# Opening an accumulation bank with its own first products, and new ranks in a list scheduler, in a four-layer attention, convolution and scan kernel

## The chip, the cores and the metric

The kernel runs on one core of a Trainium2 chip. The metric is the device time of that core in microseconds (us), as the median of several executions. "TensorE" (PE in the profile, its weight loads PEld) is the matrix engine, "VectorE" is DVE, "ScalarE" is ACT, "GpSimd" is POOL, and "SyncE" is SP.

## The reference, cut to what matters

```python
x = L0(x)   # self-attention over 4096 positions, q and k of 16 channels; gamma * out + x
x = L1(x)   # two 3x3 convolutions with 4-bit quantized weights and activations
x = L2(x)   # selective scan: 256 channels x 16 states, h = exp(dt*A)*h + dt*B*x, y = sum_n C_n*h_n,
            # gating, projection, group norm over the whole image, silu, + x
x = L3(x)   # self-attention over 4096 positions, q, k, v of 64 channels; x + wo @ out
```

There are four images of 128 channels and 64 x 64 positions. Each image passes the layers in this order, but different images can be in different layers at once. The kernel uses that: while one image is in the scan, which keeps VectorE busy, another is in an attention, which keeps TensorE and ScalarE busy.

## The kernel before

The program decides the instruction order of every engine on the host, with a list scheduler. Each piece of work is a chain (a Python generator) that yields one operation at a time with its engine, an estimated time and what it needs. The scheduler takes the operation with the smallest key and writes it out. On the chip, every engine then runs its instructions in exactly that order and waits where something is not yet there.

```python
class Order:
    LOAD, HOP, RANK = 1.3, 0.2, 0.15
    def run(self):
        ...
                load = self.LOAD if table not in (None, self.table) else 0.0
                key = start + load + self.RANK * item[0]      # item[0] is the chain's rank
                if best is None or key < best[0]:
                    best = key, start, load, item
```

So a rank is worth 0.15 us: it decides near-ties. The chains that this argument touches are these (cut):

```python
def exponentials():                  # ScalarE: p = exp(e), two halves per attention step t
    ... yield op("ACT", 1.02, ("e", t), *need, table="exp")
def decays(h):                       # ScalarE: da = exp(dt * A_n), what the scan of VectorE needs
    ... yield op("ACT", 0.7, ("dt", g), *need, table="exp")
def scans():                         # VectorE: ud*B (1.25), *C of the state before (1.22), two scans (1.26 each)
    ...
def preparation():                   # per scan group of 512 positions: products on TensorE, then on
    ...                              # ScalarE copies, silu, |x|, relu, exp, ln, with table loads
def products():                      # TensorE: values and sums of a bank
            for h in range(2):
                need = [("evict", k0 - 1)] if q == 0 and h == 0 else []
                time = (1.93 if layer == 0 else 0.95) + (0.3 if need else 0.0)
                yield op("PE", time, ("exp", t, h), *need)
                if need:
                    us = uss[k0] = ps_u.tile([P, 2, CB], F32, tag="us", name="us")   # one bank: values, sums
                    d = P if layer == 0 else 32
                    for m in range(P // d):            # the zero products
                        nc.tensor.matmul(flat(us)[m * d : (m + 1) * d, :], lhsT=w3[:, 0, m * d : (m + 1) * d],
                                         rhs=zero.to_broadcast([P, TB]), start=True, stop=False)
                ...
                        nc.tensor.matmul(us[rows, 0, :], lhsT=vts[s][:, 8 * q + k, cols],
                                         rhs=ps[t, h][:, k % 2, k // 4, :], start=False, stop=False)
            ...  # then the sums: lhsT=ones, into us[32 * m : 32 * m + 32, 1, :], start=False
```

There are 8 stages (two attentions of four images) of 16 banks and 64 attention steps t each, so 128 banks and 512 steps. The scan has 32 groups of 16 states, so 512 scan steps.

## Time and profile before

| | before |
|---|---|
| median of 3 runs | 3715.52 us (3714.67 to 3716.05) |
| profiled span | 3718.9 us |
| scan stretch: first product of the scan to the end of the last scan | 242.9 to 3361.4, 3118.5 us |
| ahead of it / after it | 242.9 us / 357.5 us |
| VectorE busy in the scan stretch | 2893.5 us, so idle for 225.0 us |

The page of the profile gives busy time per engine and, in 40 equal slices, the busy share of each in tenths. The chain that ended last follows the run back from its last instruction, each time to what released it. A view of waits has lines of the form "engine, its tile and line, <- what ended the wait: us in total, times, longest". The prediction below shows the lines of before that it reads. One more view of before, which it did not show, became the important one. It is VectorE's waits in the scan stretch:

```profile
DVE rall L647 <- PE sc L638: 66.3, 43, 3.8
DVE hs L1026 <- ACT da L991: 53.7, 34, 8.4
DVE hs L1008 <- ACT hlast L1001: 33.8, 36, 3.0
```

VectorE waits for TensorE's small products that turn the sums of attention into a column (sc), for ScalarE's decays (da), and for ScalarE's copy of the last state (hlast).

### The profile page before, as it was taken

To read this page: it belongs to the slowest core of one execution; us is meant where nothing else is said; L and a number is where in the kernel's file an instruction comes from. 1 tells how busy PE (TensorE), PEld (TensorE's weight loads), DVE (VectorE), ACT (ScalarE), POOL (GpSimd) and SP (SyncE) were. 2 spreads that over 40 slices of the span, in tenths; PEclk is the share of its full clock that TensorE was granted. 3 is DMA by queue.
4 is the path that set the end of the run, shared out by engine and by line. 5 is a ranking of instruction groups with operands and counts; after the bars stand their busy time and mean duration, and the time that the engine had idled before them with its cause. 6 is when DMAs were issued, how large, how long until landed. Compare 5 with 4: busy or idle time off the path is not lost.

```text
span 3718.9 us, 70774 instructions
## 1 busy us (share of the span) xinstructions
PE 3406.0 (92%) x29874; PEld 2235.8 (60%) x29879; DVE 3104.3 (83%) x2944; ACT 2513.0 (68%) x3656; POOL 1314.1 (35%) x568
## 2 busy tenths in 40 slices
PE   5999979989989999999888999999899989998998
PEld 3776656666666666655545666665555545565665
DVE  3369999999999999899988999999789888893333
ACT  3467767777787777777677767767777777774443
POOL 0014434444434444344433444443344444441000
PEclk8999999999999999999999999999999999999999
DMA  2023334333443334443443333343434444331000
GB/s 70 1 53 96 91 103 100 90 95 92 117 102 97 94 87 95 112 107 101 106 114 102 89 91 92 88 112 87 107 95 108 119 91 108 101 104 63 13 19 17
DMA packets 203658, 327.82 MB, mean 88 GB/s; under 512 B 50609, under 2 KB 53441, under 8 KB 203329
## 3 DMA queue, kind: packets, MB, share of 16 engines
q1 hardware_dynamic: 196384, 322.09, 34.7%
q8 instruction: 236, 3.87, 0.4%
q10 hardware_dynamic: 6944, 1.10, 0.2%
q14 instruction: 94, 0.76, 0.1%
HBM read 304.27 MB, written 18.87 MB: 87 GB/s over the span
## 4 chain that ended last, share of the span: by engine, by line
PE 61%; DVE 21%; ACT 10%; issue 5%; DMA 2%; ACTq 0%; SPq 0%; DVEq 0%
PE us L571 25%; PE e L494 14%; DVE hs L1026 9%; PE us L591 7%; DVE hs L1018 4%; DVE hs L1008 3%; PE conv L686 2%; ACT da L991 2%; ACT p L513 2%; PE xh L775 2%; PE sc L651 2%; PE yo L905 1%; PE sc L638 1%; PE proj L465 1%; PE proj L423 1%
## 5 line engine op out<-in xcount | busy, mean ns | idle before, releaser
L1043 POOL TENSOR_TENSOR y<-y,hs 128x1024 f32<-128x1024 f32 x512 | 1215.3, 2374 | 2050.1 <-DVE hs L1008 2033.6
L571 PE MATMUL us<-p,v 128*32 128x256 f32 (+1 forms) x12288 | 1521.7, 389 | 128.3 <-ACT p L513 128.1
L571 PEld LDWEIGHTS us<-p,v 128*32 128x32 f32 (+1 forms) x12288 | 1009.0, 138 | 550.1 <-ACT p L513 153.5
L513 ACT ACTIVATE p<-e 128x1024 f32<-128x1024 f32 x1024 | 1002.0, 1019 | 383.2 <-PE e L494 255.5
L1026 DVE TENSOR_TENSOR_SCAN hs<-da,hlast,hs 128x512 f32<-128x512 f32 x896 | 1102.3, 1264 | 45.5 <-ACT da L991 45.2
L991 ACT ACTIVATE da<-dt,amat 128x512 f32<-128x512 f32 x1024 | 701.1, 690 | 266.8 <-DVE hs L1026 263.0
L1008 DVE TENSOR_TENSOR hs<-hs,bc 128x1024 f32<-128x1024 f32 x512 | 666.9, 1303 | 34.7 <-ACT hlast L1001 33.8
L1018 DVE TENSOR_TENSOR hs<-ud,bc 128x1024 f32<-128x1024 f32 x512 | 656.9, 1283 | 0.0
L494 PE MATMUL e<-it,v 64*128 64x256 f32 x4096 | 534.6, 402 | 9.2 <-ACT p L513 8.2
L494 PEld LDWEIGHTS e<-it,v 64*128 64x128 f32 x4096 | 386.9, 193 | 155.6 <-issue 89.6
L591 PE MATMUL us<-p,ones 128*32 128x256 f32 x7040 | 469.9, 385 | 0.0
L591 PEld LDWEIGHTS us<-p,ones 128*32 128x32 f32 x7040 | 202.4, 110 | 183.6 <-issue 64.5
L535 DVE TENSOR_TENSOR acc<-p 128x1024 f32<-128x1024 f32 x24 | 29.4, 1225 | 225.4 <-PE us L591 192.6
L494 PEld LDWEIGHTS e<-it,j 64*128 64x128 f32 x2048 | 141.5, 190 | 101.9 <-issue 69.1
L494 PE MATMUL e<-it,j 64*128 64x256 f32 x2048 | 196.5, 310 | 5.1 <-ACT p L513 3.4
L1001 ACT COPY hlast<-hs 128x2 f32<-128x2 f32 x448 | 85.4, 191 | 130.9 <-DVE hs L1026 129.1
L535 DVE TENSOR_TENSOR acc<-p,acc 128x1024 f32<-128x1024 f32 x96 | 117.4, 1223 | 61.6 <-ACT p L513 58.1
L1026 DVE TENSOR_TENSOR_SCAN hs<-da,hs 128x512 f32<-128x512 f32 x128 | 149.9, 1204 | 8.6 <-ACT da L991 8.5
L775 PEld LDWEIGHTS <-w 128*128 128x128 bf16 x576 | 51.4, 98 | 98.3 <-issue 54.3
L775 PE MATMUL xh<-x,w 128*128 128x512 fp8e4 x384 | 95.3, 385 | 1.1 <-ACT sz L798 0.4
L1047 POOL TENSOR_TENSOR y<-y,sz 128x1024 f32<-128x1024 f32 x32 | 95.2, 2976 | 2.5
L465 PE MATMUL proj<-L_conv_wvT,x_in 128*128 128x128 f32 (+1 forms) x512 | 67.7, 288 | 22.9 <-DVE it L410 13.2
(162 smaller groups left out, 2617.3 us busy)
## 6 DMA issues: line engine op xcount, KB each, us to landing
bc<-bc_d SPq DMA_DIRECT2D x512, 512.0 KB, 4.9
x_in<-in_x SPq DMA_DIRECT2D x16, 512.0 KB, 4.8
xpad<-in_x SPq DMA_DIRECT2D x32, 256.0 KB, 3.4
x_d<-yo SPq DMA_DIRECT2D x32, 256.0 KB, 2.3
x_in<-x_d SPq DMA_DIRECT2D x16, 512.0 KB, 6.0
o<-x_d SPq DMA_DIRECT2D x32, 256.0 KB, 5.4
out<-o SPq DMA_DIRECT2D x32, 256.0 KB, 2.2
bc_d<-xd SPq DMA_DIRECT2D x64, 32.0 KB, 1.7
```

The source lines that it names most:

```text
L465: nc.tensor.matmul(to[:, k * d : (k + 1) * d], lhsT=x[:, k // 4, k % 4 * P : (k % 4 + 1) * P], rhs=wv, start=True, stop=True,)
L494: nc.tensor.matmul(e[k % 4 // 2][:, k % 2, k // 4, :], lhsT=jts[s][row : row + D3, col : col + P], rhs=its[s][row : row + D3, c * CB : (c ...
L513: nc.scalar.activation(p, es[t][h], AF.Exp)
L535: nc.vector.tensor_add(accs[k], ps[t, h], other)
L571: nc.tensor.matmul(us[rows, 0, :], lhsT=vts[s][:, 8 * q + k, cols], rhs=ps[t, h][:, k % 2, k // 4, :], start=False, stop=False,)
L591: nc.tensor.matmul(us[32 * m : 32 * m + 32, 1, :], lhsT=ones[:, 0:32], rhs=term, start=False, stop=q == NQ - 1 and k >= len(terms) - 4,)
L775: nc.tensor.matmul(g, lhsT=w3[:, k // len(rhs), lhs[k % len(rhs)] : lhs[k % len(rhs)] + P], rhs=x[:, rhs[k % len(rhs)]], start=(k == 0), s ...
L991: nc.scalar.activation(da, live["in", g][0][:, h, :], AF.Exp, scale=amat[:, h, n : n + 1])
L1008: nc.vector.tensor_mul(hs, hs, bcs.pop(m)[:, 1:2, :].to_broadcast([P, 2, TB]))
L1018: nc.vector.tensor_mul(hs, ud, bcs[m][:, 0:1, :].to_broadcast([P, 2, TB]))
L1026: nc.vector.tensor_tensor_scan(hs[:, h, :], das.pop((m, h)), hs[:, h, :], hlast[:, n, h : h + 1] if g % NTB else 0.0, ALU.mult, ALU.add,)
L1043: nc.gpsimd.tensor_tensor(y, y, hss.pop(m), ALU.add)
```

## The change

The intent is twofold. The zero products existed to clear the bank, so that all real products could add to it; now the first real products are flagged as the ones that open it. And the ranks of the chains are set anew. The constants in the scheduler change in one place, where the allowance of 0.3 us for the zero products goes.

```diff
-    zero = const.tile([P, 1], BF16, tag="zero", name="zero")
-    nc.gpsimd.memset(zero, 0.0)
...
-                time = (1.93 if layer == 0 else 0.95) + (0.3 if need else 0.0)
+                time = 1.93 if layer == 0 else 0.95
...
-                    d = P if layer == 0 else 32
-                    for m in range(P // d):
-                        nc.tensor.matmul(... rhs=zero.to_broadcast([P, TB]), start=True, stop=False)
...
-                            start=False,
+                            start=q == 0 and k < (1 if layer == 0 else 2),
...
-                order.add(1, copy(o, flat(g), key, 1.2))        # in two places
+                order.add(4, copy(o, flat(g), key, 1.2))
-                order.add(1, stage_input(s))
+                order.add(5, stage_input(s))
-                    order.add(1, residual(b, c))
-                order.add(0, finish(s, c, us, ss))
+                    order.add(-1, residual(b, c))
+                order.add(2, finish(s, c, us, ss))
...
             (1, parts()),
-            (1, convolutions()),
-            (1, preparation()),
-            (1, output()),
+            (3, convolutions()),
+            (2, preparation()),
+            (3, output()),
             (1, lasts()),
             (3, energies()),
-            (4, exponentials()),
+            (2, exponentials()),
             (4, products()),
-            (3, decays(0)),
-            (3, decays(1)),
+            (1, decays(0)),
+            (1, decays(1)),
             (3, scans()),
-            (3, additions()),
-            (3, fetches()),
-            (1, accumulations()),
-            (3, images()),
+            (6, additions()),
+            (2, fetches()),
+            (-2, accumulations()),
+            (5, images()),
```

More of the change, by code (lines that the diff above doesn't have):

```diff
@@ L472, in operands @@
             mark(*key, "in")
-            order.add(1, copy(o, flat(g) if layer == 0 else g, key, 1.2))
+            order.add(4, copy(o, flat(g) if layer == 0 else g, key, 1.2))
         return freed + lows
@@ L550, in products @@
                     us = uss[k0] = ps_u.tile([P, 2, CB], F32, tag="us", name="us")
-                    d = P if layer == 0 else 32
-                    for m in range(P // d):
-                        nc.tensor.matmul(
-                            flat(us)[m * d : (m + 1) * d, :],
-                            lhsT=w3[:, 0, m * d : (m + 1) * d],
-                            rhs=zero.to_broadcast([P, TB]),
-                            start=True,
-                            stop=False,
-                        )
                 for k in range(2 * h, 2 * h + 6):
```

## The prediction

> **What bounds the kernel now.** I read the page's busy shares first, then its forty slices, the chain that ended last, then waits and the order of time.
>
> ```profile
> PE 3406.0 (92%) x29874; PEld 2235.8 (60%) x29879; DVE 3104.3 (83%) x2944; ACT 2513.0 (68%) x3656; POOL 1314.1 (35%) x568
> ...
> PE   5999979989989999999888999999899989998998
> ...
> DVE  3369999999999999899988999999789888893333
> ...
> PE 61%; DVE 21%; ACT 10%; issue 5%; DMA 2%; ACTq 0%; SPq 0%; DVEq 0%
> ```
>
> No engine is full all the time. Slices 1 to 3 and the last four are TensorE's alone: the attention of image 0 before a scan can start, and the second attention of image 3, which needs the last scan. Between them, from about 243 us (first scan product) to 3360 us, TensorE and VectorE are both near 93%: summing the windows from 260 to 3360, VectorE works 2875 of 3100 us. Neither is saturated. The instructions of each engine are in a fixed order, and an engine stalls where the engine it waits for is not as far as the order supposed. The waits of TensorE from 260 to 3360 us show where:
>
> ```profile
> PE us L571 <- ACT p L513: 124.6, 38, 12.7
> PE us L553 <- ACT ss L619: 24.1, 28, 1.8
> PE z L775 <- ACT sz L798: 21.0, 16, 2.8
> ```
>
> The first, the product of values waiting for its exponential, is half of TensorE's 250 us of waiting there. In order of time, such a wait at 2933 us:
>
> ```profile
> 2929.34 1.05 ACT L875 ACTIVATE sp<-sp 128x1024 f32<-128x1024 f32 x1
> 2930.43 1.06 ACT L877 ACTIVATE y<-sp 128x1024 f32<-128x1024 f32 x1
> 2931.39 0.18 ACT L1001 COPY hlast<-hs 128x2 f32<-128x2 f32 x1
> 2931.47 0.68 ACT L991 ACTIVATE da<-dt,amat 128x512 f32<-128x512 f32 x1
> 2932.10 1.91 ACT L513 ACTIVATE p<-e 128x1024 f32<-128x1024 f32 x2
> ...
> 2933.15 1.93 PE L571 MATMUL us<-p,v 128*32 128x256 f32 x16 [5.00 <-ACT p L513]
> ```
>
> ScalarE was never idle; it ran the preparation of a scan group (table load, copies, absolute value, exponential) ahead of the attention's exponential. This recurs about once per group of 32. So the cause is the order on ScalarE, which is what the new ranks rearrange.
>
> **What the Trainium skill says.** "PSUM — Partial Sum Buffer", The four PSUM rules: the first product of a group, flagged as such, clears the written-bits of the whole 2 KiB bank over the quadrants it writes; later products without the flag overwrite where a bit is clear and add where it is set. The bank here is 2 x 256 floats, 2 KiB, holding values and sums. So one flagged product on all rows (layer 0), or four on 32 rows each (layer 3), opens both halves, and the zero products are superfluous. No trace of before shows this; correctness of the changed kernel will. "TensorE: Matmul & The Clock Gate", Back-to-back issue gap, gives about 216 ns for 512 columns; and its Part 3 says products in different column tiles run concurrently. This trace agrees with both:
>
> ```profile
> 2264.11 0.38 PE L553 MATMUL us<-zero,w 128*128 128x512 bf16 x1
> 2264.33 1.89 PE L571 MATMUL us<-p,v 128*128 128x256 f32 x8
> ...
> 1655.59 0.40 PE L553 MATMUL us<-zero,w 128*32 128x512 bf16 x4
> 1655.81 1.03 PE L571 MATMUL us<-p,v 128*32 128x256 f32 x16
> ```
>
> The next product starts 0.22 us after one zero product of layer 0, and also 0.22 us after four of layer 3. The busy total of that line (48.4 us) counts overlapped pipeline time, so it is not the cost. "ScalarE: Activation LUTs", What ACT_TABLE_LOAD costs, has about 2.7 us for a table load; every one here took 1.283 us, and that decides.
>
> **The change, part by part.** I compared the instruction order that each kernel builds, and weighted the matmuls with the spacing of their starts in this trace.
>
> *Zero products.* There are 8 stages of 16 banks, so 128 x 0.22 = 28.2 us leave TensorE: 112 banks (24.6 us) ahead of the last output product of the scan, 16 (3.5 us) in the last attention. The wait for the bank's eviction (24.1 us) does not go: the first real product inherits it. TensorE's stream falls from 3295 to 3267 us by my weights.
>
> *Ranks.* The scheduler chooses the operation with the smallest start plus 0.15 us times rank, so ranks settle near-ties. The exponentials go from 4 to 2, level with preparation (1 to 2); decays from 3 to 1, ahead of it; convolutions and output fall to 3. Every count of work stays. Table loads on ScalarE in the main part: 137 before, 136 after, so 1.3 us, nothing.
>
> What the order shows moved: ahead of the last output product TensorE issues energies for 443 of 512 attention steps instead of 447, and products for five steps fewer. A layer-3 step costs 4.65 us (its energy groups start at 1645.77 and 1650.42 us). Four energies at 1.93, five products at 1.86 and five sums at 0.9 us are 21.5 us taken out of the shared stretch and put after it. With 24.6 us of zeros, 46 us less TensorE work stands before the last scan output.
>
> What follows that output:
>
> ```profile
> 3383.45 1.13 PE L670 MATMUL o<-us,wo 128*128 128x512 f32 x2 [0.85 <-DVE us L659]
> 3393.33 3.78 PE L423 MATMUL proj<-x_in,L_conv_wkTr 128*128 128x512 f32 x4 [8.76 <-DMA x_in<-x_d]
> ```
>
> Image 3's normalization and its trip through memory leave TensorE idle 8.76 us. The five postponed steps fit there in part: the output product ended near 3370.0 and the projection began 23.3 us later, with 14.6 us of work. With 21.5 us more, the projection can start at the earliest some 36 to 37 us after the output, and the idle gap goes.
>
> *Sum with waiting unchanged.* Last output: 3370.0 - 46 = 3324. Projection: + 37 = 3361. Rest: 3718.9 - 3393.3 = 325.6, less 3.5 of zeros = 322. Span 3683 us, about 3680 in the timed runs (whose median is 3.4 us below the profiled span): 1.0% faster.
>
> *What the order does to waiting.* Between consecutive instructions of attention exponentials on ScalarE I summed the other work (durations of this trace). Work beyond 3 us in such a stretch: 596 us before, 543 after; stretches of 12 us or more fall from 22 to 12. For the decays that feed the scan, the same excess is 409 against 384. So TensorE starves less often behind preparation, and VectorE behind decays. I do not take all of it: half of the first difference (26 us), my choice, as TensorE often has other work queued, and none of the second, since it lies beside the first. That gives 3680 - 26 = 3654, rounded to 3655 us (1.6%).
>
> The start is slightly worse: 2 us more TensorE work stands before the first scan group's products. The last attention is spread more evenly (products no longer come five half-steps in a row), but in before a pair of banks took 36.64 us there, with 36.7 us of work by my weights, so only the zeros can shorten it.
>
> **Rivals.** (a) VectorE paces the middle. It must do the same 2875 us; to keep up with 46 us less TensorE work its idle time must fall from 225 to under 180. For it: 93 to 97% in most windows of 200 us from 560 to 2560 us, and scan rows run longer (1283 and 1303 ns) than the 1.25 and 1.22 us the scheduler supposes. Against: only 85 to 93% from 1760 to 2160 and from 2560 to 3160 us, where layer-3 attention runs, and 66 us of its waiting is for TensorE's small transposing products, which come sooner. If true, the zeros turn into waiting and only the gap at the end remains: 3695 to 3715. (b) The new ranks merely move the stalls: exponentials earlier delay preparation, so scans start later at group boundaries. For it: preparation loses priority against decays. Against: long gaps between decays don't grow. It would make 3680 to 3710. (c) The ranks remove most of the 125 us wait and the decays' starvation as well: a 60 to 80 us gain beyond the zeros, 3600 to 3635. For it: ranks are set anew only after trying, and TensorE's granted clock (0.92 to 0.96 in the windows where it stalls most, 0.99 to 1.0 where it doesn't) rises as stalls go.
>
> **Range and chances.** The sure part is 28 us, the structural sum 36, the likely centre 60, with a tail to 100 by (c) and to 10 by (a). That gives 3605 to 3700. Over 2% means under 3641: 33%. Slower by over 2% needs a new stall of 75 us with less work: 3%.
>
> **What would show it.** In the changed profile: no zero products; TensorE busy lower by 25 to 48 us; the product's wait for exponentials in the middle at about 100 us instead of 125; the idle gap before the last projection under 5 us, about 36 us after the last output product; that product near 3300; the last attention at 36.2 us per pair of banks; VectorE's idle time in its middle stretch below 180 us. The prediction is wrong if VectorE's idle stays at 225 us (rival a), if a new releaser tops TensorE's waits (b), or if the wait for exponentials falls under 80 us (c).

One sentence is cut from it, since the page section that it named for the time of a table load does not say that. Its sum does not change: the 1.3 us for one table load fewer is the trace's, where every table load took 1.283 us.

## The result, and the profile after

The changed kernel takes **3650.81 us** (median of 4 runs, 3647.95 to 3653.8), against 3715.78 us for the kernel before in the same rounds. The ratio is 0.9823, with a 95% interval of 0.9806 to 0.9840. Ratios here are the mean time of one kernel's fast runs over the mean of the other's fast runs of the same rounds, so not quite the ratio of the medians. By the threshold of 2% this counts as the same; the interval shows a gain of 1.6 to 1.9%. The result is correct, so the first flagged products do open both halves of the bank.

The page of the changed kernel, with the lines for engines, TensorE's and VectorE's slices, and the chain (line numbers from the products on are 11 lower than before, in the exponentials 2 lower):

```profile
PE 3375.5 (92%) x29559; PEld 2217.0 (61%) x29559; DVE 3124.9 (86%) x2944; ACT 2505.9 (69%) x3655; POOL 1317.5 (36%) x567
...
PE   5999989999999899999988999999989999999998
...
DVE  3369999999999999999999999999989999982333
...
PE 50%; DVE 32%; ACT 9%; issue 6%; DMA 2%; ACTq 0%; DVEq 0%; SPq 0%
```

TensorE loses 30.5 us of busy time, but its share stays at 92%. VectorE's share rises from 83 to 86%, and its part of the chain rises from 21 to 32%. Of the dips to 7 and 8 tenths that VectorE's slices had in the second half of the scan, one slice of 8 is left.

Next is one line of the view by windows for the scan stretch of each kernel, first of before, then of after. The columns are the stretch and its length, then the busy time (and number of instructions) of PE, PEld, DVE, ACT and POOL, then TensorE's granted clock, the DMA share and GB/s.

```profile
242.90:3361.40 3118.50, 2877.85 (x24681) 1881.15 (x24687) 2893.54 (x2666) 2249.84 (x3347) 1305.67 (x542) 0.97 0.40 99
```

```profile
241.00:3275.40 3034.40, 2823.08 (x24099) 1844.45 (x24101) 2911.30 (x2662) 2231.44 (x3333) 1309.15 (x542) 0.97 0.41 102
```

The scan stretch is 84.1 us shorter, although VectorE is busy in it for 17.8 us longer, with about as many instructions (2662 against 2666). VectorE's idle time falls from 225.0 to 123.1 us. Ahead of the stretch 1.9 us are gained, and after it 19.1 us are given back (376.6 us instead of 357.5). The sum, -1.9 - 84.1 + 19.1, is the difference of the two profiled spans, 66.9 us.

VectorE's waits in the scan stretch of the changed kernel:

```profile
DVE rall L636 <- PE sc L627: 45.1, 39, 3.2
DVE hs L1015 <- ACT da L980: 18.3, 15, 3.0
DVE hs L997 <- ACT hlast L990: 15.5, 22, 1.6
```

All three are shorter, and the two for ScalarE fall together by 53.7 us (from 87.5 to 33.8). TensorE's longest waits from 260 to 3310 us:

```profile
PE us L560 <- ACT p L511: 71.2, 28, 6.5
PE us L560 <- ACT ss L608: 26.2, 25, 2.8
```

The wait for exponentials was 124.6 us. The wait for the eviction of the bank, which the zero products had (24.1 us), is now that of the first real product, 26.2 us: it was inherited, as predicted. In order of time, ScalarE around a group's preparation (from 2851 us) now looks like this:

```profile
2851.18 1.00 ACT L511 ACTIVATE p<-e 128x1024 f32<-128x1024 f32 x1
2852.08 0.58 ACT L787 ACTIVATE sz<-z 128x512 f32<-128x512 f32 x1
2852.56 1.02 ACT L511 ACTIVATE p<-e 128x1024 f32<-128x1024 f32 x1
2853.99 0.69 ACT L980 ACTIVATE da<-dt,amat 128x512 f32<-128x512 f32 x1 [0.41 <-DVE hs L1015]
2854.62 0.58 ACT L787 ACTIVATE sz<-z 128x512 f32<-128x512 f32 x1
2855.17 0.20 ACT L990 COPY hlast<-hs 128x2 f32<-128x2 f32 x1
2855.27 0.69 ACT L980 ACTIVATE da<-dt,amat 128x512 f32<-128x512 f32 x1
```

An exponential (p), a preparation step (sz) and a decay (da) take turns. This is another part of the preparation than the one that the prediction shows at 2929 us, but that part changed likewise. From its table load at 2918.86 us to 2932.10 us, the kernel before ran no exponential. The changed kernel ran four in the same part of that group's preparation (table load at 2873.16 us, steps to 2892 us): two at 2880.30 and two at 2885.42.

### The profile page after: what moved, and what is told of

The parts are those of the page before. It is cut to its first block, busy times and chain, and to the rows that moved or that the text cites. A ratio compares the mean times of both kernels' runs of the same rounds, so it can differ in the third digit from the quotient of the medians.

```text
span 3652.0 us, 70191 instructions
## 1 busy us (share of the span) xinstructions
PE 3375.5 (92%) x29559; PEld 2217.0 (61%) x29559; DVE 3124.9 (86%) x2944; ACT 2505.9 (69%) x3655; POOL 1317.5 (36%) x567
## 4 chain that ended last, share of the span: by engine, by line
PE 50%; DVE 32%; ACT 9%; issue 6%; DMA 2%; ACTq 0%; DVEq 0%; SPq 0%
PE us L560 21%; DVE hs L1015 13%; PE e L492 12%; DVE hs L1007 7%; PE us L580 6%; DVE hs L997 5%; ACT da L980 2%; ACT p L511 2%; PE proj L463 2%; PE conv L675 1%; PE xh L764 1%; PE proj L421 1%; PE sc L627 1%; PE yo L894 1%; PE sc L640 1%
## 5 line engine op out<-in xcount | busy, mean ns | idle before, releaser
L463 PE MATMUL proj<-L_conv_wvT,x_in 128*128 128x128 f32 (+1 forms) x512 | 71.3, 298 | 27.5 <-DVE it L408 17.8
```

What stands on the lines that cost most here:

```text
L463: nc.tensor.matmul(to[:, k * d : (k + 1) * d], lhsT=x[:, k // 4, k % 4 * P : (k % 4 + 1) * P], rhs=wv, start=True, stop=True,)
```

## The experiments

The total came within 5 us of the predicted 3655. That doesn't show that the parts were right. The main theory was that TensorE's work is on the path, so that the zero products are worth 20 to 28 us and the order some 36. The rival A said that VectorE paces the scan stretch, so that the zeros are mostly hidden and the order is everything. All times quoted are of fast runs. Where kernels of different rounds are compared, I compare their ratios to the kernel before in their own rounds.

### The two parts apart: four kernels on one chip

The first has the kernel before's instruction order (the scheduler's operations, times and ranks are untouched) and no zero products:

```diff
                 time = (1.93 if layer == 0 else 0.95) + (0.3 if need else 0.0)     # kept
-                    (zero products)
-                            start=False,
+                            start=q == 0 and k < (1 if layer == 0 else 2),
```

> The kernel before, its instruction order kept to the letter (old ranks, the old 0.3 us allowance for the zero products in the scheduler), only the zero products gone. Theory (TensorE is on the chain most of the time): 20 to 28 of the 28.2 us show, 3690 us. Rival A (VectorE paces the middle stretch, zeros there are hidden): only the zeros ahead of the first scan and after the last one show, 5 to 10 us, 3707 us. Rival C (the zeros are everything, the ranks nothing): 65 us, 3651 us.

It took 3708.0 us (10 runs), ratio 0.9976 (0.9967 to 0.9986), so about 9 us by the ratio. That is rival A's size, not the theory's 20 to 28 us. The second drops the 0.3 us allowance as well, so that the scheduler computes a new order with the old ranks:

```diff
-                time = (1.93 if layer == 0 else 0.95) + (0.3 if need else 0.0)
+                time = 1.93 if layer == 0 else 0.95
```

> Old ranks, zero products gone and their 0.3 us allowance gone too, so the scheduler sets a new order. Theory: as the first run, 3690 us, within 10 us, since the ranks that decide near-ties are the old ones. Rival A: 3707 us. Rival D (any newly computed order without the allowance is as good as the new ranks): 3650 to 3660 us.

It took 3717.36 us, ratio 1.0011 (1.0003 to 1.0019). With 28 us less TensorE work it is no faster than the kernel before: the newly computed order lost what the zeros had given. So rival D, that any new order would do, falls. The third is the opposite, new ranks with the zero products and their allowance:

```diff
 (the kernel before, with only the ranks of the change)
```

> New ranks, zero products and their allowance of 0.3 us kept. Theory: the order is worth 36 us, 3680 us, with the wait of products for exponentials near 75 us as in the changed kernel. Rival A: the order is worth nearly all, 3655 to 3665 us. Rival C: 3715 us.

It took 3664.79 us, ratio 0.9855 (0.9838 to 0.9871): the ranks alone are worth about 54 us by the ratio. That is what rival A expected (3655 to 3665 us), not the theory (3680 us). The fourth is the changed kernel, order kept, with the zeros put back:

```diff
+                    (zero products)
-                            start=q == 0 and k < (1 if layer == 0 else 2),
+                            start=False,
```

> The changed kernel, its instruction order kept to the letter, with the zero products put back in. Theory: 20 to 28 us slower than the changed kernel, 3671 to 3679 us. Rival A (in the new order VectorE paces the middle): 5 to 10 us slower, 3657 us.

It took 3660.64 us, ratio 0.9855 (0.9841 to 0.9868), some 10 to 12 us slower than the changed kernel (9.8 by the medians, 0.0032 of 3716 us by the ratios), at the upper end of rival A's range and half of the theory's. The two profiled runs differ by 5.6 us only, and show where these 5.6 us lie. The line for its scan stretch:

```profile
243.60:3278.27 3034.67, 2831.84 (x24335) 1850.81 (x24337) 2911.22 (x2662) 2232.40 (x3333) 1311.01 (x542) 0.98 0.41 102
```

The stretch is 3034.7 us with the zeros and 3034.4 without, and VectorE's busy time in it is the same to 0.1 us. In these two runs the zeros within the scan stretch are hidden. What they cost lies ahead of it (2.6 us) and after it (2.7 us), where TensorE works alone. The other 4 to 6 us of the difference between the medians or ratios is not located by any profile; some of it may lie in the stretch.

### Which ranks

The next kernel starts from the second experiment (3717.36 us) and takes over only the ranks of five chains that compete on ScalarE (the copies of the projections run there too, and keep their old rank):

```diff
-            (1, convolutions()), (1, preparation()), (1, output()),
+            (3, convolutions()), (2, preparation()), (3, output()),
-            (4, exponentials()), (3, decays(0)), (3, decays(1)),
+            (2, exponentials()), (1, decays(0)), (1, decays(1)),
```

> From the kernel with the zero products out and old ranks (3717 us), only the ranks of the chains that compete on ScalarE set anew: preparation 2, exponentials 2, decays 1, convolutions 3, output 3. Theory S (VectorE paces the scan stretch and lost its time waiting for ScalarE's decays and state copies): at least 40 of the 66 us between that kernel and the changed one come back, 3650 to 3677 us, with VectorE's wait for decays under 25 us. Rival F (the gain is in VectorE's own order, in the finish chain, the additions and the accumulations): under 20 us, 3697 us or more.

It took 3655.76 us, ratio 0.9842 (0.9828 to 0.9855). From 1.0011 to 0.9842 is 0.0169, of the 0.0188 to the changed kernel's 0.9823: about nine tenths of what the new ranks give come from these chains. The intervals of this kernel and of the changed one overlap, so the remaining tenth is not shown. VectorE's waits from 260 to 3260 us:

```profile
DVE rall L636 <- PE sc L627: 54.1, 41, 13.2
DVE us L648 <- PE sc L640: 21.2, 32, 2.1
DVE hs L997 <- ACT hlast L990: 15.8, 19, 2.6
DVE hs L1015 <- ACT da L980: 15.4, 16, 2.9
```

The waits for ScalarE are as in the changed kernel; those for TensorE's small products are not. This kernel's span divides otherwise, too: its scan stretch is 3053.6 us, longer than the changed kernel's, and 351.2 us follow it, because no attention step of image 2 is left over (448 of 512 steps precede the last output product, against 443). The same time can be reached by different divisions. One rank undone, in the changed kernel:

```diff
-            (1, decays(0)), (1, decays(1)),
+            (3, decays(0)), (3, decays(1)),
```

> The changed kernel with one thing undone: decays back at rank 3, behind preparation and the exponentials on ScalarE. Theory S: this rank is the main one, 30 us or more are lost, 3680 to 3710 us, and VectorE's wait for decays goes from 18 back to 45 us or more. Rival F: within 10 us of the changed kernel, 3651 to 3661 us.

It took 3795.06 us, ratio 1.0216 (1.0202 to 1.0230), slower even than the kernel before. VectorE's longest wait from 260 to 3260 us:

```profile
DVE hs L1015 <- ACT da L980: 158.4, 64, 10.1
```

It was 18.3 us. With decays at 3 and exponentials and preparation at 2, VectorE starves for decays. The loss of 144 us was far more than the 30 to 60 us expected. TensorE's wait for exponentials, from which the prediction read the gain, shrank in this slowest kernel of all, from 65.2 us in the same window to this:

```profile
PE us L560 <- ACT p L511: 19.0, 15, 3.1
```

So a shorter wait of TensorE is not by itself a gain. The last kernel of the study asked the reverse, whether that one rank carries the gain by itself, from the second experiment:

```diff
-            (3, decays(0)), (3, decays(1)),
+            (1, decays(0)), (1, decays(1)),
```

> The kernel with the zero products out and old ranks (3717 us), with one thing changed: decays from rank 3 to 1, level with the other chains on ScalarE. If the decays' rank alone carries the gain: 3656 to 3675 us, VectorE's wait for decays under 25 us, down from 48. If it needs the exponentials' and preparation's new places with it: 3690 us or more, with TensorE's wait for exponentials at 130 us or higher, since the decays are then paid for by the exponentials.

It took 3736.82 us, ratio 1.0061 (1.0047 to 1.0075), slower than where it started. So the rank does not act alone. The expected reason was only half met. The scan stretch became shorter (3097.8 us, from 3117.3), but 396.2 us follow it instead of 354.1. With decays first and exponentials left at 4, attention falls behind: 438 steps precede the last output product, 446 did. TensorE's wait for exponentials was 109.1 us, not the 130 or more that I had written; the loss shows as attention left over. VectorE's waits for decays fell from 48.0 to 31.2 us, but for state copies they rose from 33.1 to 55.8. It is the relation of the ranks on ScalarE that counts, not one of them. Decays have to come ahead of exponentials and preparation, and that is not enough while the exponentials stay at 4. How much of the rest is due to exponentials moved forward, to preparation moved back, or to convolutions and output put behind was not tested apart.

### What paces the scan stretch

If VectorE paced it alone, less VectorE work would show in full. These kernels compute something else on purpose. In the first pair every fourth multiplication by C is done on half its columns, in the old order without zeros and in the changed kernel:

```diff
-        nc.vector.tensor_mul(hs, hs, bcs.pop(m)[:, 1:2, :].to_broadcast([P, 2, TB]))
+        w = 1 if m % 4 == 0 else 2
+        nc.vector.tensor_mul(hs[:, 0:w], hs[:, 0:w], bcs.pop(m)[:, 1:2, :].to_broadcast([P, w, TB]))
```

> Wrong result on purpose. The first experiment's kernel (old order, zeros out, 3708 us) with every fourth multiplication by C on 128x512 instead of 128x1024: 128 times some 0.6 us, about 78 us less VectorE work, same order. If VectorE paces the scan stretch: 45 to 78 us faster, 3630 to 3663 us. If TensorE paces it (the prediction's main line): under 25 us faster, 3683 us or more.

> Wrong result on purpose. The changed kernel (3651 us) with the same 78 us less VectorE work. If VectorE paces the scan stretch of the new order too: 45 to 78 us faster, 3573 to 3606 us; its share of the gain should then be at least that in the old order. If TensorE takes over at once: under 25 us faster, 3626 us or more.

They took 3667.92 us (ratio 0.9871), between the two expectations, and 3626.45 us (0.9761), at the edge of the one for TensorE. Both passed the comparison with the reference, so that comparison does not see this fault. In the second pair a part of the sum products is left out of the same two kernels, which the comparison did reject, as it should:

```diff
+            if t % 3 == 0 and len(terms) == 8:
+                terms = terms[4:]
             for k, term in enumerate(terms):
```

> Wrong result on purpose. The first experiment's kernel (old order, zeros out, 3708 us) with 139 of the sum products of the middle halved (four of eight products left out), by the rows of before some 0.45 us each, 62 us less TensorE work, same order. Taking out the zeros from this order shortened the scan stretch by 15 of 25 us, so if TensorE paces the old order: 30 to 45 us faster, 3663 to 3678 us. If VectorE does: under 15 us, 3693 us or more.

> Wrong result on purpose. The changed kernel (3651 us) with the same 62 us less TensorE work, same order. Putting the zeros back lengthened the scan stretch of this order by 0.3 us only, so if VectorE paces it, with TensorE now running ahead: under 12 us faster, 3639 us or more. If TensorE paces it as much as in the old order: 30 to 45 us faster, 3606 to 3621 us.

They took 3688.66 us (0.9935), between the two expectations, and 3643.76 us (0.9802), within the one for VectorE. These are the lines of the scan stretch: the old order without zeros, then with VectorE and with TensorE lighter; and the new order with VectorE and with TensorE lighter (its starting kernel is shown above).

```profile
242.40:3346.07 3103.67, 2852.89 (x24441) 1864.19 (x24443) 2893.94 (x2667) 2250.85 (x3347) 1305.88 (x542) 0.97 0.40 100
241.50:3312.17 3070.67, 2844.78 (x24437) 1862.23 (x24439) 2826.53 (x2666) 2246.18 (x3347) 1306.38 (x542) 0.97 0.39 101
241.30:3332.07 3090.77, 2808.76 (x23349) 1833.96 (x23351) 2892.11 (x2666) 2249.49 (x3347) 1305.13 (x542) 0.96 0.39 100
```

```profile
240.90:3245.67 3004.77, 2817.52 (x24092) 1842.23 (x24093) 2840.35 (x2663) 2229.21 (x3333) 1310.15 (x542) 0.98 0.39 103
242.40:3269.37 3026.97, 2781.32 (x23022) 1817.77 (x23023) 2908.19 (x2662) 2230.93 (x3334) 1311.00 (x542) 0.97 0.39 102
```

The table gives how much less busy the engine was in the stretch, how much shorter the stretch became in these profiles, and how much shorter the whole time became by the ratios of all fast runs, each against its own starting kernel. The last column is the safer one: the profiled run of the old order without zeros is the fastest of its ten (3702.0 us, median 3708.0), that of the changed kernel the slowest of its four. It is uncertain by some 7 to 8 us, by the intervals of the ratios.

| order, engine lightened | less busy | stretch shorter | whole time shorter |
|---|---|---|---|
| old, VectorE | 67.4 us | 33.0 us (49%) | 39 us (58%) |
| old, TensorE | 44.1 us | 12.9 us (29%) | 15 us (34%) |
| new, VectorE | 70.9 us | 29.6 us (42%) | 23 us (32%) |
| new, TensorE | 41.7 us | 7.4 us (18%) | 8 us (19%) |

In either order only a part of the work taken out shows: a third to three fifths of VectorE's, a fifth to a third of TensorE's. Neither theory holds as written. No engine paces the stretch alone: what does not show turns into waiting of the lightened engine for another, since the order is fixed. VectorE's work counts for more than TensorE's in the old order. In the new order both seem to count for less, and there the difference between the two shares is within the uncertainty. The chain that ended last agrees: it moves away from the engine that was lightened. In the new order TensorE has 50% of it and VectorE 32%. That becomes 59% and 24% with VectorE lighter, and with TensorE lighter this:

```profile
PE 40%; DVE 40%; ACT 8%; issue 8%; DMA 3%; POOL 0%; ACTq 0%; SPq 0%; DVEq 0%; POOLq 0%
```

### A step further

The largest of VectorE's waits left is the reciprocal's for the small products (45.1 us). The scheduler sets the reciprocal right behind them by its own estimate. In the changed kernel, I told it that they arrive 1.5 us later, which puts more scan work in between:

```diff
-        yield op("PE", 0.65, bank=True)
+        yield op("PE", 0.65, bank=True, lag=1.5)
         sc = gtile("sc")
 ...
-        yield op("DVE", 0.18)
+        mark("sc", n)
+        yield op("DVE", 0.18, ("sc", n))
```

> The changed kernel with the scheduler told that the small column products which turn the sums arrive 1.5 us later, so that VectorE's reciprocal, its largest wait left (45 us in 39 waits), is set behind more scan work. If VectorE paces the scan stretch, that wait falls under 20 us and 10 to 25 us are gained, 3626 to 3641 us. If the later finish holds the shared bank and TensorE's next work back instead: 3651 to 3670 us.

It took 3641.88 us (3636.94 to 3644.73, 5 runs), ratio 0.9805 (0.9791 to 0.9818), and is correct. VectorE's waits from 260 to 3260 us:

```profile
DVE hs L1016 <- ACT da L981: 31.0, 20, 5.3
DVE us L649 <- PE sc L641: 17.8, 14, 6.0
...
DVE rall L637 <- PE sc L627: 1.9, 4, 0.6
```

The wait is gone, 1.9 us instead of 45.1; a part came back in the decays and in the multiplication that follows. Against the changed kernel this is 9 us by the medians, below the 10 to 25 us expected. The two were not run in the same rounds and their intervals overlap, so I call the gain over the changed kernel likely, not shown. Over the kernel before, it is shown.

## Why the prediction was right or wrong

**The total and the range were right:** 3651 us measured, 3655 predicted, in the range. **The composition was not.** Two terms of its sum were off, in opposite directions, by similar amounts.

- **The term of 28.2 us for zero products was mis-sized.** The step that failed is the sum "with waiting unchanged", which put all of TensorE's saved work on the path. Taking the zeros out of the old order gave about 9 us, and putting them back into the new one cost 10 to 12. The cost of one bank (0.22 us of TensorE's stream) may well be right, as the starts in the trace say; what failed is where it lies. In the new order the zero products of 102 banks, some 22 us, lay inside the scan stretch and changed its length by 0.3 us in the two profiled runs.
- **The rest, from the order, was too small.** The prediction had 34 us: some 8 from the idle gap ahead of the last projection, and 26, half of what the listing of ScalarE suggested, from fewer starving products. The ranks alone gave about 54 us. The prediction read the cause at the right place (the order on ScalarE, where preparation ran in blocks), but gave nothing for the decays, whose share "lies beside the first". It did not: VectorE's two waits for ScalarE fell by 53.7 us, and with the decays alone put back the time rose to 3795 us. TensorE's wait for exponentials fell from 124.6 to 71.2 us, by all of the 53 us that the listing suggested and not by half. This is below the 100 predicted and below the 80 under which the prediction called itself wrong in the sense of rival (c).
- **Rival (a)** was right that zeros are mostly hidden, and wrong that nothing then remains: VectorE's idle time fell to 123 us, under the 180 given as the mark. It was idle for want of decays and state copies, and better order on ScalarE gave it these. **Rival (c)** had the mechanism nearest to what happened, though not the size. **Rival (b)** did not happen in the changed kernel. The experiment with decays put back shows a stall that was merely moved, though to the decays and not to the preparation that this rival named.
- **Confirmed steps:** the inherited wait for eviction (26.2 us); 1 table load fewer; TensorE's busy time 30.5 us lower; the last attention at 36.05 us per pair of banks (products of the output at 3435.63, 3471.68 and 3507.73 us), 36.2 predicted. What follows the last output product of the scan grew by 14 us (from 348.9 to 363.1), where the prediction's sum had 10 (37 us to the projection instead of 23.3, less 3.5 of zeros).
- **Small misses:** the last output product ended at 3288.8 us, 3298 by the prediction's sum. The last projection began 42.7 us after that instead of 36 to 37. The idle gap before the projection is gone, but a wait of 5.98 us for exponentials behind image 3's silu took its place:

```profile
3309.45 1.94 PE L560 MATMUL us<-p,v 128*32 128x256 f32 x16 [5.98 <-ACT p L511]
```

- **Two readings of before were too neat.** Of the windows in which VectorE is less busy, that from 1960 to 2160 us is mostly layer 0, not layer 3 (products of layer 3 end at 1988 us and start again at 2521). And TensorE's granted clock was 0.95 to 1.00 in the windows where it stalls little, not 0.99 to 1.0: from 1160 to 1360 us it was 0.95, with TensorE busy for 188.6 of 200 us. Over the whole profiled runs the clock did go with the stalls: 0.967 before, 0.974 in the changed kernel, 0.952 with decays put back.

What stays open: how much of the 54 us is the decays' and how much the exponentials' share. In these runs the gain came only where both moved, and moving the decays alone made things worse, so a division may not exist. Whether the other ranks give the remaining tenth is not shown.

## What to carry to other kernels

Where two engines are both near 93% in a fixed instruction order, work removed from one of them is only in part time removed (here a fifth to three fifths): measure what the removal is worth by taking it out with the order kept, before counting on it. Look at the engine that feeds both (here ScalarE, busy for 68%): the order of its instructions decided more than the work of either. And judge the terms of a prediction one by one, since a right total can hide two errors that cancel.

## What the Trainium skill lacked or had wrong

- "ScalarE: Activation LUTs": its section What ACT_TABLE_LOAD costs gives 1283 ns for the load and, with a drain of some 1380 ns, about 2.66 us for every switch of tables; its Terms give about 2.7 us for the load itself. All table loads in the trace of before took 1283 ns. From the end of the instruction before a load to the start of the one behind it there were 1.31 us (median of 142), so the trace shows no such drain.
- "TensorE: Matmul & The Clock Gate", Back-to-back issue gap, gives about 216 ns for 512 columns as the gap of an isolated product, and about 131 ns as the spacing in a sustained stream. In the trace of before the zero products (0.22 us to the next start) and the products z and xh of the scan's preparation (512 columns, 216 ns from start to start, median of 448) came at the isolated gap in the midst of the stream.
- No page read for this case says how little of such a gap may show where a second engine is as busy: 128 of them, 28.2 us, changed the time by 9 to 12 us.
- "PSUM — Partial Sum Buffer", The four PSUM rules, says that a flagged product clears the whole bank over the quadrants that it writes. All seven kernels without zero products that keep the arithmetic were correct, and the comparison does see faults in these sums (it rejected the two with sum products left out, relative error 0.22). This agrees; nothing to mend.
